# A transformer block on one core: the order of key units, values in two halves, and pinned row statistics

## The chip, the cores and the metric

The kernel runs on one core of one Trainium2 chip. The time is that of the device for one execution, in microseconds (us). Before the change it was run three times: 3664.93, 3666.43 and 3667.56 us, a median of 3666.43. A further execution was taken by the hardware profiler: 3665.12 us, of which 3663.4 us are the span that its trace covers.

A core has five engines that work through their own instruction streams in order and wait for one another by semaphores. TensorE (PE in the trace; PEld are its weight loads) multiplies matrices into banks of PSUM. VectorE (DVE) and ScalarE (ACT) work on rows of 128 partitions, GpSimd (POOL) as well, and SyncE (SP) here issues DMA transfers.

## The reference

The input h has 8 batch elements of 1024 tokens with 512 features, in float32. The block is an attention and a feed-forward layer, each between layer norms:

```python
x = h
x = x + layernorm(attention(layernorm(x)))
x = x + layernorm(ffn(layernorm(x)))

def attention(h):                      # 16 heads of 32
    q, v, k = split(h @ Wqvk)
    scores = q @ k.T                   # causal: a key after its query is masked
    return softmax(scores / sqrt(512)) @ v @ Wo

def ffn(x):                            # 512 -> 2048 -> 512
    hidden = x @ W1 + b1
    imag = w_imag * sin(theta + hidden * 0.1)
    phase = cos(theta) * w_real + sin(theta) * w_imag
    return relu(hidden + phase * imag * 0.1) @ W2 + b2
```

The means and variances of the layer norms are taken over the 512 features of a token (a row).

## The kernel before

**Outer order.** A loop runs over the 8 batch elements b. For each there are four attention groups g of four heads (`attention`, L867 to L971), then the end of the attention block for the second half of the tokens, interleaved with the feed-forward layer (`feed_forward`, from L1050). The feed-forward takes 8 steps: four quarters of the hidden features for each half of 512 tokens. Its products, the output projection's neighbours and the query and key projections of groups 1 to 3 use seven products in place of eight (Strassen and Winograd forms); POOL mixes operands for them, and mixed weights are kept in DRAM (`w1_mixed`, `w2_mixed`, `qk_mixed`). In the first batch element POOL also mixes these weights while attention runs.

**What sets the order.** Most instructions are issued through `in_order`, which pins an instruction in its engine's program order; one that goes through `id` instead, or through nothing, may be moved by the scheduler. The work is written as Python generators that issue a piece at each step: `advance(gen)` issues one piece, `finish(gen)` the rest. So the place of an `advance` call in the code is the place of that piece among the work of every engine that it uses. `staged(n, *stages)` gives a generator for n tiles through several stages, with tile t in stage k at step t + k. At each step the later stages come first.

**PSUM and buffers.** `psum()` hands out the 8 banks, preferring the one drained longest ago. The pool `pp` holds 24 tiles of 128x1024 f32 (keys, queries, values, weights of the softmax), `tmp` 5 tiles of 128x512, `wp` 18 tiles of weights.

**An attention group.** `project_qkv(b, g)` is a generator that makes a group's values, queries and keys. The values come in four pieces of two token tiles (`values`, L525 to L539: 8 matmuls to a tile of 128 tokens and 4 feature blocks in L530, then one ACT copy of 128x256 in L538). The first piece, `values(0)`, is issued in the previous group; the rest fills gaps in `find_maxima`, by the numbers in MAX_FILL. `find_maxima` computes the row maxima of the scores (L673 on PE, then L691 or L703 on DVE, with exponentials L723 on ACT). They are transposed (L913 copies the second half's to SBUF).

Then come the weights. For the two halves c of the queries, `KEY_UNITS[c]` lists units, each one or two blocks of 128 keys. For a unit, `weigh` puts minus the maxima (L779) and then the scores (L790) in PSUM on PE, takes the exponential on ACT (L805, two tiles) and, for a block on the diagonal of the causal mask, zeroes what lies above it with a select on POOL (L809). In the second half (c = 1) blocks 4 to 7 are those on the diagonal, so that the units (4), (5,7) and (6) need selects. The widths of queries are 512 for blocks 0 to 4, and 384, 256 and 128 for 5, 6 and 7.

A step behind it (`late`), PE multiplies the weights with the values (L828). In the second half the weights of all units are also added up on DVE in two tiles (`add_weights`, L857) into those of unit (0), and after the last unit PE sums these over the keys (L843) and ACT and DVE divide (L862 to L865). In group 3 the last two units are left out of the addition (`apart`) and summed on PE. At the last but one unit of c = 1 the group's projections are finished and the next group's first piece is issued (L916 to L919):

```python
if c and u == len(units) - 2:
    finish(work)
    work = projections(g + 1)
    advance(work)
```

Creating and starting a projection also allocates q, k and v in `pp` and issues its five weight fetches on SP.

**The norms.** `moments` (L309, L310) are the row statistics on DVE, `rstd_of` (L316, L317) two short POOL instructions, `normalised` (L328) one DVE instruction. For batch element b + 2, `measure_ahead` (L438 to L460) takes the statistics of the input x, tile by tile, during the last two feed-forward steps of b (by MEASURE). `norm1` uses them in group 2 of the element after. `finish_block` (L974 to L1046) projects the attention's output (L1005 on PE, a copy L1014 on ACT), takes its statistics, normalises and adds it to x (L1021), takes the statistics of x, scales it (L328 again, tile xn), transposes it on PE (L114) and mixes operands for the feed-forward on POOL (L1041). For the first half of the tokens this happens in group 3, for the second in the first three feed-forward steps, where `BETWEEN` says at which quarter-steps a stage is advanced.

**The feed-forward.** A step's hidden block comes from L1117 on PE, with additions on DVE (L1187) and copies on ACT (L1191, L1200). Then `wave_in` (L1138, L1143, L1144 on DVE, the sine L1145 on ACT) and `wave_out` (L1160, L1166 on DVE) form the wave, POOL mixes it (hm, L1233), and the second product (L1252 on PE) with additions (L1264, tile yb) makes the output. `end` (L1322 to L1351) finishes two tiles of output rows: POOL adds b2 (L1333), then in stages `measure`, `add` (L328 and L1343) and `store`. The last of these ends is left to the next element's group 0 and advanced there once a unit (`rest`).

Of the kernel before, what the change touches and what calls it, by code (L numbers as in the profile page):

```python
# [16 lines left out]
P = 128  # L17
# [15 lines left out]
def kernel(  # L33
# [14 lines left out]
    nc = tc.nc  # L48
# [257 lines left out]
    def moments(src, mv, keep=id):  # L306

        st = small.tile([P, 6], F32, tag="st", name="st", bufs=3)
        keep(nc.vector.bn_stats(st, src))  # L309
        keep(nc.vector.bn_aggr(mv, st))  # L310
# [127 lines left out]
    def measure_ahead(b, steps):  # L438


        xs = {}
        mvs = small.tile([P, NT, 2], F32, tag="mva", name="mva", bufs=1)
        rss = small.tile([P, NT], F32, tag="rsa", name="rsa", bufs=1)
        moments_ahead[b] = mvs, rss
        at = [sum(steps[:n]) for n in range(len(steps) + 1)] + [NT]

        def load(n):
            for t in range(at[n], at[n + 1]):
                xs[t] = load_again(b, t)

        load(0)
        load(1)
        yield True
        for n in range(len(steps)):
            for t in range(at[n], at[n + 1]):
                moments(xs.pop(t), mvs[:, t, :], in_order if b == 1 else id)
            if n + 2 < len(steps):
                load(n + 2)
            if n == len(steps) - 1:
                rstd_of(mvs, NT, rss)  # L460
            yield True
# [35 lines left out]
    def project_qkv(b, g):  # L497
# [24 lines left out]
            in_order(nc.scalar.activation(dst, pq, AF.Copy, scale=HALF_SCALE if n else -HALF_SCALE))  # L522
            drained(pq)

        def values(t0):  # L525
            pv = psum([P, 2, P])
            for t in (t0, t0 + 1):
                for kc in range(KC):
                    in_order(
                        nc.tensor.matmul(  # L530
                            pv[:, t - t0, :],
                            xnT[b, t // TPB][:, kc, (t % TPB) * P : (t % TPB + 1) * P],
                            w_of[b, g, 1][:, kc, :],
                            start=(kc == 0),
                            stop=(kc == KC - 1),
                        )
                    )
            in_order(nc.scalar.copy(v[b, g][:, t0 : t0 + 2, :], pv))  # L538
            drained(pv)  # L539

        def product(w, kc0, moving, dst, sign=1.0):
# [56 lines left out]
                values(t0)  # L598
                yield True

        values(0)
        yield True
        values(2)
        yield True
# [19 lines left out]
    MAX_LATE = (((7, 1),), ((7, 0),))  # L624


    MAX_FILL = ((2, 1, 1, 1), (1, 1, 1, 1))

    KEY_UNITS = (
        ((0,), (1, 3), (2,)),  # L630
        ((0,), (1,), (2,), (3,), (4,), (5, 7), (6,)),
    )

    def find_maxima(b, g, work, sums, more):
# [233 lines left out]
    def attention(b, wvT, after):  # L868
# [23 lines left out]
        for g in range(NG):  # L892
# [7 lines left out]
            for c in range(2):  # L900
# [3 lines left out]
                for u, keys in enumerate(units):  # L904
# [5 lines left out]
                    if at == 2:  # L910
# [2 lines left out]
                                parts_q[1], lambda *a: in_order(nc.vector.tensor_copy(*a))  # L913
                            )
                        )
                    if c and u == len(units) - 2:  # L916
                        finish(work)
                        work = projections(g + 1)
                        advance(work)  # L919
                    if first is None and (at < 2 or c and u >= len(units) - 2):  # L920
                        advance(more)
# [54 lines left out]
    def finish_block(b, half, wvT, x2T, mixed, out_w):  # L976
# [13 lines left out]

        def measure(t, source):
            mvs[t] = one_mv()
            moments(source, mvs[t][:, 0, :])
            if half:
                rss[t] = rstd_of(mvs[t], 1)

# [26 lines left out]
        def scale(t):  # L1023
            deviation(t)
            xns[t] = tmp.tile([P, D], F32, tag="tmp", name="xn")
            normalised(xns[t], x(t), mvs[t], rss[t])

        def transpose(t):
            transpose_rows(xns[t], x2T[half][:, :, t * P : (t + 1) * P], nc.scalar.copy)
# [20 lines left out]
    def feed_forward(b, x2T, mixed, before, between):  # L1050
# [14 lines left out]
            (1, 2, 1, 3),  # L1065
            (7,) * 6,
        )
        BETWEEN = ((0, 1, 2, 4), (1, 3), (3,))
        MEASURE = {STEPS - 1: 2, STEPS: 7}
        hids = {}  # L1070
        ahead = []
# [250 lines left out]
        def end(half, q, ybs):  # L1322
# [11 lines left out]

            def measure(t):
                mvs[t] = one_mv()
                last = (half, q) == (1, 1)
                moments(ybs[t], mvs[t][:, 0, :], in_order if last else id)
                rss[t] = rstd_of(mvs[t], 1)

            def add(t):
# [6 lines left out]
                if b + 1 < B:  # L1348
                    load_x(b + 1, i)

            return staged(len(ybs), measure, add, store)  # L1351

        def advance_ends(steps):
            for _ in range(steps):
# [116 lines left out]
```

## Time and profile before

| | |
|---|---|
| median of three runs | 3666.43 us (3664.93 to 3667.56) |
| the profiled execution | 3665.12 us, span 3663.4 us |
| granted TensorE clock, mean | 0.997 |
| instructions | 62,023 |
| busiest group of PE: L1117 from x2T, 2048 matmuls | 477.2 us |
| busiest group of DVE: L857, 400 additions | 423.7 us, mean 1.105 us |
| busiest group of ACT: L805, 640 exponentials | 566.1 us, mean 0.938 us |
| busiest group of POOL: L809, 512 selects | 291.7 us, mean 0.590 us |

A batch element in the middle takes about 451 us. The stretches of batch element 3, from the profile by windows (us from the start of the span; the busy times of the engines within each):

| stretch | window | PE | DVE | ACT | POOL | DMA share |
|---|---|---|---|---|---|---|
| end of the feed-forward before | 1381 to 1410.81 | 29.71 | 13.77 | 2.03 | 18.85 | 0.94 |
| group 0 | 1410.81 to 1468 | 56.76 | 44.94 | 34.27 | 32.04 | 0.25 |
| group 1 | 1468 to 1522 | 53.77 | 40.52 | 34.79 | 19.37 | 0.15 |
| group 2 | 1522 to 1575 | 52.77 | 42.43 | 37.21 | 20.47 | 0.15 |
| group 3 and first projections | 1575 to 1650 | 73.69 | 48.99 | 41.35 | 11.57 | 0.04 |
| entry of the feed-forward | 1650 to 1680 | 28.30 | 21.23 | 6.91 | 10.42 | 0.42 |
| feed-forward | 1680 to 1797 | 116.71 | 91.13 | 18.98 | 41.80 | 0.73 |
| its last two steps | 1797 to 1832 | 32.77 | 31.10 | 5.29 | 16.79 | 0.79 |

How to read it: a matmul's time runs to its modelled end and overlaps the next one's, so a stretch in which PE is busy nearly throughout can still hold matmuls that waited. In a line of the timeline the columns are start, duration, engine, line of the kernel, operation, tiles out<-in, shapes, how many of them in a row, and in brackets the idle time of the engine before them with what ended it. Four matmuls over 32 rows (the four heads of a group) run side by side on PE.

### The profile page before, as it was taken

The page shows a single profiled execution, that of the slowest core. Times are in us where ns is not written, and L with a number is a line of the kernel's source. Part 1 is how long each engine was busy: PE and PEld are TensorE (multiplying, and loading weights), DVE is VectorE, ACT ScalarE, POOL GpSimd, SP SyncE. Part 2 cuts the span into 40 slices and gives each one's busy share as a digit, 9 for nine tenths or more (in the row PEclk, how much of TensorE's full clock was granted, in tenths as well). Part 3 has the DMA queues.
Part 4 walks back from the last instruction along what each step waited for, and adds up shares of the span by engine and source line. Part 5 has one row for each costly group of instructions (what it writes and reads, how often), then busy time and mean ns, then how long its engine had stood idle before and what let it go on. Part 6 is the DMA issues. An engine that isn't in the chain of part 4 may idle for free.

```text
span 3663.4 us, 62023 instructions
## 1 busy us (share of the span) xinstructions
PE 3574.9 (98%) x22625; PEld 2342.6 (64%) x22625; DVE 2698.7 (74%) x5571; ACT 1449.6 (40%) x2780; POOL 1434.5 (39%) x1984
## 2 busy tenths in 40 slices
PE   8999999999999999999999999999999999999998
PEld 4447864478654786448864488544885548854587
DVE  5877768778686786767867677776777767777675
ACT  4553136621365214652146511464115642156310
POOL 5543453134541345313453234542344323443243
PEclk9999999999999999999999999999999999999999
DMA  4444761047610575105841068410683116720175
GB/s 139 159 142 121 247 204 47 21 137 246 196 47 16 153 252 173 53 10 168 262 148 53 13 181 268 126 53 17 197 275 105 47 35 198 262 81 19 52 220 194
DMA packets 312001, 488.83 MB, mean 133 GB/s; under 512 B 29904, under 2 KB 91408, under 8 KB 311696
## 3 DMA queue, kind: packets, MB, share of 16 engines
q1 hardware_dynamic: 309536, 483.02, 41.8%
q8 instruction: 180, 2.95, 0.3%
q10 hardware_dynamic: 2160, 1.84, 0.2%
q14 instruction: 125, 1.02, 0.1%
HBM read 451.71 MB, written 33.03 MB: 132 GB/s over the span
## 4 chain that ended last, share of the span: by engine, by line
PE 81%; DVE 11%; POOL 3%; ACT 2%; issue 1%; DMA 0%; SPq 0%; POOLq 0%; DVEq 0%; ACTq 0%
PE banks L1252 16%; PE banks L1117 15%; PE banks L545 8%; PE banks L673 8%; PE banks L828 6%; PE banks L790 6%; PE banks L530 6%; PE banks L1005 6%; PE banks L513 3%; PE banks L779 3%; PE banks L114 2%; DVE u L1144 2%; DVE hid L1160 2%; PE banks L843 1%; ACT w L805 1%
## 5 line engine op out<-in xcount | busy, mean ns | idle before, releaser
L805 ACT ACTIVATE w<-banks 128x1024 f32<-128x1024 f32 (+1 forms) x640 | 566.1, 938 | 259.4 <-PE banks L790 258.7
L857 DVE TENSOR_TENSOR w<-w 128x1024 f32<-128x1024 f32 (+3 forms) x400 | 423.7, 1105 | 182.8 <-PE banks L828 138.4
L809 POOL TENSOR_SCALAR_AFFINE_SELECT w<-w 128x256 f32<-128x256 f32 x512 | 291.7, 590 | 674.0 <-ACT w L805 666.2
L1117 PE MATMUL banks<-x2T,wm 128*128 128x256 f32 x2048 | 477.2, 381 | 28.2 <-DVE u L1187 13.6
L703 DVE CUSTOM_DVE_ANT_0 es<-banks,mask 128x128 f32<-128x128 f32 (+3 forms) x1024 | 432.2, 484 | 61.6 <-PE banks L673 61.6
L1252 PE MATMUL banks<-wm,hm 128*128 128x256 f32 x2048 | 470.3, 380 | 2.3 <-POOL hm L1233 2.3
L1145 ACT ACTIVATE u<-u 128x1024 f32<-128x1024 f32 x128 | 135.4, 1058 | 846.8 <-DVE u L1144 798.1
L1117 PEld LDWEIGHTS banks<-x2T,wm 128*128 128x128 f32 x2048 | 386.6, 190 | 91.1 <-DVE u L1187 16.8
L1252 PEld LDWEIGHTS banks<-wm,hm 128*128 128x128 f32 x2048 | 387.9, 190 | 56.5 <-POOL hm L1233 5.5
L691 DVE TENSOR_REDUCE mx<-banks 128x1 f32<-128x512 f32 (+1 forms) x384 | 309.8, 862 | 120.1 <-PE banks L673 119.8
L1233 POOL TENSOR_TENSOR hm<-hid 128x256 f32<-128x256 f32 x256 | 203.5, 795 | 448.8 <-DVE hid L1166 448.8
L1252 PE MATMUL banks<-wm,hid 128*128 128x256 f32 x1536 | 357.7, 379 | 0.0
L828 PE MATMUL banks<-w,v 128*32 128x512 f32 (+3 forms) x3072 | 322.9, 496 | 9.6 <-POOL w L809 9.6
L790 PE MATMUL banks<-q,k 32*128 32x512 f32 (+3 forms) x3072 | 330.9, 492 | 0.0
L673 PE MATMUL banks<-k,q 32*128 32x512 f32 (+3 forms) x3072 | 325.4, 513 | 0.4 <-DVE mx L703 0.2
L1252 PEld LDWEIGHTS banks<-wm,hid 128*128 128x128 f32 x1536 | 292.3, 190 | 39.2
L723 ACT ACTIVATE es<-es,mx 128x512 f32<-128x512 f32 (+3 forms) x512 | 279.7, 551 | 1.8 <-DVE mx L703 1.8
L530 PEld LDWEIGHTS banks<-wqvk,xnT 128*128 128x128 f32 x2048 | 238.5, 192 | 50.1 <-issue 25.4
L530 PE MATMUL banks<-wqvk,xnT 128*128 128x128 f32 x2048 | 260.3, 281 | 0.0
L673 PEld LDWEIGHTS banks<-k,q 32*128 32x128 f32 x3072 | 149.9, 185 | 146.9 <-DVE mx L703 66.9
L1117 PE MATMUL banks<-mix,wm 128*128 128x256 f32 x1024 | 241.9, 379 | 0.0
L1005 PE MATMUL banks<-wo,wvT 128*128 128x512 f32 x512 | 235.7, 601 | 3.2 <-DVE wvT L865 3.2
(135 smaller groups left out, 5074.1 us busy)
## 6 DMA issues: line engine op xcount, KB each, us to landing
wm<-w_mixed SPq DMA_DIRECT2D x1344, 256.0 KB, 3.1
xin<-in_L_attn_h_dram SPq DMA_DIRECT2D x112, 256.0 KB, 3.9
wqvk<-in_L_attn_Wqvk_dram SPq DMA_DIRECT2D x93, 256.0 KB, 5.4
out_dram<-x SPq DMA_DIRECT2D x64, 256.0 KB, 2.3
x<-in_L_attn_h_dram SPq DMA_DIRECT2D x60, 256.0 KB, 3.3
w_mixed<-w_t SPq DMA_DIRECT2D x56, 256.0 KB, 3.0
wmix<-qk_mixed SPq DMA_DIRECT2D x42, 256.0 KB, 5.1
wo<-in_L_attn_Wo_dram SPq DMA_DIRECT2D x32, 256.0 KB, 2.7
```

What stands on the lines that cost most here:

```text
L530: nc.tensor.matmul(pv[:, t - t0, :], xnT[b, t // TPB][:, kc, (t % TPB) * P : (t % TPB + 1) * P], w_of[b, g, 1][:, kc, :], start=(kc == 0), ...
L545: nc.tensor.matmul(pq, w[:, kc0 + kc, :], moving[:, kc, :], start=kc == 0, stop=kc == 1,)
L673: nc.tensor.matmul(scs[j // 2][:, j % 2, at : at + n], queries[r, i * P : (i + 1) * P], keys[r, k0 : k0 + n], start=True, stop=True,)
L691: nc.vector.tensor_reduce(out=mx[:, m], in_=sc[:, m, cols], op=ALU.min, axis=mybir.AxisListType.X,)
L703: nc.vector.tensor_tensor_reduce(out=es[:, m, cols], in0=sc[:, m, cols], in1=mask[:, HALF - n :], scale=1.0, scalar=FMAX, op0=ALU.add, op1 ...
L790: nc.tensor.matmul(sts[j // 2][:, j % 2, cols], all_keys[r, kb * P : (kb + 1) * P], all_queries[r, q0 : q0 + n], start=False, stop=True,)
L805: in_order(nc.scalar.activation(w[:, :, :width], st[:, :, :width], AF.Exp, scale=-1.0))
L828: nc.tensor.matmul(acc[r, HALF - n :], v[b, g][:, kb, r], weights[j // 2][:, j % 2, cols], start=first and k == 0, stop=last and k == len( ...
L857: in_order(nc.vector.tensor_add(t[:, :, q], t[:, :, q], w[:, :, cols]))
L1005: nc.tensor.matmul(y, wvT[:, kc, t * P : (t + 1) * P], out_w[kc], start=(kc == 0), stop=(kc == KC - 1),)
L1117: nc.tensor.matmul(bank[:, n, :], w[:, n, kc, :], moving[:, kc, :], start=first and kc == 0 and n == 0, stop=kc == 1 and n == 1, skip_grou ...
L1252: nc.tensor.matmul(region, a[:, n], w[:, n], start=start and n == 0, stop=last and n == 1, skip_group_check=True,)
```

## The change

- `measure_ahead` pins its statistics for every batch element, where before it did so only for b = 1.
- The first values piece of two token tiles, `values(0)`, becomes two pieces of one tile each, `values(0, 1)` and `values(1, 1)`. A projection has nine pieces instead of eight. MAX_FILL for group 0 takes three pieces first instead of two.
- The units of the second half are put in the order (0), (4), (1), (5,7), (2), (6), (3).
- The previous projection is finished, and the next one created and its first piece issued, after unit (0) of the second half. The second piece follows at the last but one unit.
- In `finish_block` the second half's statistics are pinned, and so is the scaling (L328) of that half. The stages between the feed-forward's pieces (`BETWEEN`) are put at other places over the first three steps.
- In `end` the first stage does nothing. The statistics are taken one step later, and are pinned always.

```diff
@@ -453,7 +453,7 @@
         yield True
         for n in range(len(steps)):
             for t in range(at[n], at[n + 1]):
-                moments(xs.pop(t), mvs[:, t, :], in_order if b == 1 else id)
+                moments(xs.pop(t), mvs[:, t, :], in_order)
             if n + 2 < len(steps):
                 load(n + 2)
             if n == len(steps) - 1:
@@ -522,9 +522,9 @@
             in_order(nc.scalar.activation(dst, pq, AF.Copy, scale=HALF_SCALE if n else -HALF_SCALE))
             drained(pq)
 
-        def values(t0):
-            pv = psum([P, 2, P])
-            for t in (t0, t0 + 1):
+        def values(t0, n=2):
+            pv = psum([P, n, P])
+            for t in range(t0, t0 + n):
                 for kc in range(KC):
                     in_order(
                         nc.tensor.matmul(
@@ -535,7 +535,7 @@
                             stop=(kc == KC - 1),
                         )
                     )
-            in_order(nc.scalar.copy(v[b, g][:, t0 : t0 + 2, :], pv))
+            in_order(nc.scalar.copy(v[b, g][:, t0 : t0 + n, :], pv))
             drained(pv)
 
         def product(w, kc0, moving, dst, sign=1.0):
@@ -598,7 +598,9 @@
                 values(t0)
                 yield True
 
-        values(0)
+        values(0, 1)
+        yield True
+        values(1, 1)
         yield True
         values(2)
         yield True
@@ -624,11 +626,11 @@
     MAX_LATE = (((7, 1),), ((7, 0),))
 
 
-    MAX_FILL = ((2, 1, 1, 1), (1, 1, 1, 1))
+    MAX_FILL = ((3, 1, 1, 1), (1, 1, 1, 1))
 
     KEY_UNITS = (
         ((0,), (1, 3), (2,)),
-        ((0,), (1,), (2,), (3,), (4,), (5, 7), (6,)),
+        ((0,), (4,), (1,), (5, 7), (2,), (6,), (3,)),
     )
 
     def find_maxima(b, g, work, sums, more):
@@ -913,9 +915,11 @@
                                 parts_q[1], lambda *a: in_order(nc.vector.tensor_copy(*a))
                             )
                         )
-                    if c and u == len(units) - 2:
+                    if c and u == 0:
                         finish(work)
                         work = projections(g + 1)
+                        advance(work)
+                    if c and u == len(units) - 2:
                         advance(work)
                     if first is None and (at < 2 or c and u >= len(units) - 2):
                         advance(more)
@@ -990,7 +994,7 @@
 
         def measure(t, source):
             mvs[t] = one_mv()
-            moments(source, mvs[t][:, 0, :])
+            moments(source, mvs[t][:, 0, :], in_order if half else id)
             if half:
                 rss[t] = rstd_of(mvs[t], 1)
 
@@ -1023,7 +1027,9 @@
         def scale(t):
             deviation(t)
             xns[t] = tmp.tile([P, D], F32, tag="tmp", name="xn")
-            normalised(xns[t], x(t), mvs[t], rss[t])
+            scaled = normalised(xns[t], x(t), mvs[t], rss[t])
+            if half:
+                in_order(scaled)
 
         def transpose(t):
             transpose_rows(xns[t], x2T[half][:, :, t * P : (t + 1) * P], nc.scalar.copy)
@@ -1065,7 +1071,7 @@
             (1, 2, 1, 3),
             (7,) * 6,
         )
-        BETWEEN = ((0, 1, 2, 4), (1, 3), (3,))
+        BETWEEN = ((0, 1, 2), (0, 2), (1, 3))
         MEASURE = {STEPS - 1: 2, STEPS: 7}
         hids = {}
         ahead = []
@@ -1334,8 +1340,7 @@
 
             def measure(t):
                 mvs[t] = one_mv()
-                last = (half, q) == (1, 1)
-                moments(ybs[t], mvs[t][:, 0, :], in_order if last else id)
+                moments(ybs[t], mvs[t][:, 0, :], in_order)
                 rss[t] = rstd_of(mvs[t], 1)
 
             def add(t):
@@ -1348,7 +1353,7 @@
                 if b + 1 < B:
                     load_x(b + 1, i)
 
-            return staged(len(ybs), measure, add, store)
+            return staged(len(ybs), lambda t: None, measure, add, store)
 
         def advance_ends(steps):
             for _ in range(steps):
```

On the engines this makes 32 matmuls fewer on PE (the sums of group 3: units (6) and (3) stand last there now), 32 ACT copies more (one of 128x128 twice for one of 128x256 in each of the 32 groups), and on DVE 240 additions of 128x1024 instead of 256, with 64 instead of 48 each of the forms of unit (5,7).

## The prediction

> **What bounds the kernel now.** I read the busy shares and the chain first, to see whether one engine sets the end.
>
> ```profile
> PE 3574.9 (98%) x22625; PEld 2342.6 (64%) x22625; DVE 2698.7 (74%) x5571; ACT 1449.6 (40%) x2780; POOL 1434.5 (39%) x1984
> PE 81%; DVE 11%; POOL 3%; ACT 2%; issue 1%; DMA 0%; SPq 0%; POOLq 0%; DVEq 0%; ACTq 0%
> ```
>
> TensorE (PE) is busy 98% and holds 81% of the chain at a granted clock of 0.997. The change takes no PE work away, so only the places where PE stands still can give anything. The list of PE's waits names them (line waited on, total us, times, longest):
>
> ```profile
> PE banks L1117 <- DVE u L1187: 15.9, 16, 1.7
> ...
> PE banks L828 <- POOL w L809: 9.6, 12, 2.4
> PE banks L1117 <- ACT p L1191: 9.2, 6, 1.5
> PE banks L779 <- ACT w L805: 8.7, 33, 1.0
> ```
>
> The whole list is 75 us, 9 of them one wait at the start. More stall hides inside busy matmuls that start late. Set against the same groups running freely, a batch element of 451 us loses some 14.5 us. The timeline of batch element 3 shows where, first at the end of its feed-forward (start, us, engine, line, idle before):
>
> ```profile
> 1805.76 1.03 PE L1252 MATMUL banks<-wm,hid 128*128 128x256 f32 x4
> 1808.31 3.72 PE L1117 MATMUL banks<-x2T,wm 128*128 128x256 f32 x16 [1.52 <-ACT p L1191]
> ...
> 1818.64 1.99 PE L1117 MATMUL banks<-x2T,wm 128*128 128x256 f32 x8 [0.57 <-DVE hid L1187]
> ...
> 1832.14 2.21 PE L1252 MATMUL banks<-wm,hm 128*128 128x256 f32 x9 [0.29 <-POOL hm L1233]
> ```
>
> With the late starts beside them PE loses 1.79, 0.83 and 0.56 us here, 3.2 in all. VectorE (DVE) at that time:
>
> ```profile
> 1799.19 0.69 DVE L309 BATCH_NORM_STATS2 st<-yb 128x6 f32<-128x512 f32 x1 [1.38 <-POOL yb L1333]
> ...
> 1802.53 0.69 DVE L309 BATCH_NORM_STATS2 st<-xin 128x6 f32<-128x512 f32 x1
> ...
> 1804.30 0.66 DVE L309 BATCH_NORM_STATS2 st<-xin 128x6 f32<-128x512 f32 x1
> 1804.88 1.76 DVE L1144 TENSOR_TENSOR u<-u,k 128x1024 f32<-128x1024 f32 x1
> ```
>
> Row statistics of y (waiting 1.38 for POOL) and of later inputs stand in front of the sine chain (L1138 to L1166) that PE waits for. Nobody needs those statistics soon. The second place is the start of the next element's group 0, where DVE's first maximum (L703) stands behind another statistic:
>
> ```profile
> 1411.74 0.70 DVE L309 BATCH_NORM_STATS2 st<-yb 128x6 f32<-128x512 f32 x1 [1.38 <-POOL yb L1333]
> ...
> 1412.57 0.26 DVE L703 CUSTOM_DVE_ANT_0 es<-banks,mask 128x128 f32<-128x128 f32 x1
> ```
>
> PE's 16 score matmuls at 1414.25 then take 3.10 us to the next group (1417.35) instead of 1.93. The third place is the end of each attention group; group 1:
>
> ```profile
> 1503.87 6.90 DVE L857 TENSOR_TENSOR w<-w 128x1024 f32<-128x1024 f32 x6 [5.12 <-PE banks L828]
> 1511.23 1.23 DVE L857 TENSOR_TENSOR w<-w 128x1024 f32<-128x1024 f32 x1 [0.45 <-POOL w L809]
> 1512.75 1.23 DVE L857 TENSOR_TENSOR w<-w 128x1024 f32<-128x1024 f32 x1 [0.30 <-POOL w L809]
> 1514.28 4.70 DVE L857 TENSOR_TENSOR w<-w 128x768 f32<-128x768 f32 x6 [0.30 <-POOL w L809]
> ```
>
> and POOL's selects there:
>
> ```profile
> 1510.79 0.41 POOL L809 TENSOR_SCALAR_AFFINE_SELECT w<-w 128x256 f32<-128x256 f32 x1 [11.30 <-ACT w L805]
> 1511.70 1.02 POOL L809 TENSOR_SCALAR_AFFINE_SELECT w<-w 128x256 f32<-128x256 f32 x1 [0.51 <-ACT w L805]
> ```
>
> The 14 additions take nearly all of 1503.87 to 1518.98; the weight sums (L843) need the last, and the next group starts on PE at 1520.02, 1.04 behind it. So the tail is a chain of additions, not of PE.
>
> **The change, part by part.** Durations are those of this profiled execution, 3665.12 us, 1.31 below the median and inside the runs' spread; I add the sum to the median.
>
> *Statistics at the feed-forward's end.* Those of the inputs (4 × about 0.85: L309 0.67 and L310 0.18, so 3.4 us of DVE) now follow the last wave stage, and those of y come a step later, behind POOL's addition of 1.27. The last hidden block is done at 1830.42 now. From 3.4 us and the 1.38 wait only what PE waits for counts, at most 3.2. The third stall is cured when the block comes 2.1 earlier; the first is partly ACT's copy of p (0.57, behind a 1.06 activation), so some 1 us remains. I take −2.1 (−1.0 to −2.6) in elements 0 to 5, and −1.0 in 6 and 7, which measure no inputs: −14.6.
>
> *Start of group 0.* No y statistic is ahead of the maxima; an input's may be, but that has no wait. 3.10 − 1.93 = 1.17, in 7 elements: −8.2. The cover is DVE being free: if the input statistics (8 × 0.85 at most) reach that far, the whole gain goes.
>
> *Group 0, second half.* Here the statistics, normalisation and addition that moved must still run: L309 and L310 0.88, L328 0.54, L1343 0.69, twice, less what overlaps and what stands here today. All 3.2 us now lie between additions. The first additions are those of unit (4), which need exponentials and selects: unit (0) leaves PE at 1446.60 and the additions start 3.76 later; with the values' first half (8 matmuls, about 1.0) and a select of 0.41 in between, 4.40. Then 13.55 of additions, 3.2 and gaps of 0.7: last addition at 21.85, weight sums at about 22.75, where today the next group starts at 20.57 (1467.17). +2.15 (1.9 to 2.4) in 7 elements: +15. What waits: the weight sums, then the next group's second values, first scores and maxima.
>
> *Groups 1 and 2.* The values' 1.0 us fills PE's stop behind unit (0) (0.9 with the late start), a gain; but products of units (4) and (5,7) now meet a select 0.41 to 1.02 long with less PE work ahead: +0.8 and +0.75. Group 1 from 1500.34: PE's own work 17.83, with these and 0.18 more 19.6, the additions' chain 18.5 + 1.04 = 19.5; late halves add up, so I take 20.1 against 19.68: +0.45 (0 to +0.8), 8 times, +3.6. In group 2 the next input's two normalisations (0.5 each) fall between the additions of (2) and (6): +0.85 (0 to +1.5), 7 elements: +6.1.
>
> *Group 3.* Units (6),(3) are summed by PE instead of (5,7),(6). That is 32 matmuls fewer in all, but 256 + 512 columns as 384 + 128 + 256 before: nothing. DVE adds 0.6 us more early on, hidden by some 2 us free between units. The normalised rows (L328) stand earlier in DVE's order, so the 0.69 wait at 1643.69 goes: −0.8 (−1 to +0.5), 8 times: −6.4.
>
> *Entry of the feed-forward.* Pinned statistics and scaling, with norm steps shifted, let the second step's u come at 1676.9 instead of 1678.54, but the third near 1682: of the 2.0 us stop, −0.55 (−1.2 to +0.5), 8 times: −4.4.
>
> *Costed at nothing.* 16 values matmuls as 8 and 8 take 1.98 either way. ACT has 32 more copies (0.37 for a full one; ACT is 40% busy). SP's five weight fetches per group go out five units earlier; in these stretches the DMA share is 0.15, nothing is queued behind them, and they land in a median 5.4 us. If no buffer were free then, SP would hold the stores and loads behind them. Element 0 has no earlier feed-forward and POOL mixes weights there: 0 ± 4.
>
> Sum: −14.6 − 8.2 − 6.4 − 4.4 + 15 + 3.6 + 6.1 = −8.9: **3657 us**. This case's own range is 3648 to 3668.
>
> A select takes 0.41 alone and 1.02 when it meets an addition (it ends 0.26 behind it). [...]
>
> **The rivals.**
> - *The tails cost little* (the additions slide into today's gaps). For it: DVE idles about 5 us before them in group 1. Against: the chain has under 1.1 us of gaps. Losses of 0.3 × 22 leave −27: 3639. Chance 0.20.
> - *Slower: selects and additions hold each other up.* Place: additions of (4) to (6) in groups 0 to 2. For it: under weight mixing in element 0 selects take 1.29 to 1.44 and additions 1.42 to 2.29. Against: in group 1 today additions beside selects take 1.23, like all others. Six additions by 1.42 − 1.22 give 1.2 a group, 22 groups, +26: 3683. It decides from 0.4 a group. Chance 0.26.
> - *The statistics were not the stall:* ACT's p and POOL's hm hold PE at the feed-forward's end. For it: the 1.52 wait names ACT. Against: that p waited for DVE's 1.76 addition. A gain of 0.5 instead of 2.1 or 1.0 there loses 10.6: 3668. Chance 0.14.
>
> **How the numbers follow.** 0.40 is left for my forecast. A measurement tells from no change about 0.2%, 7.3 us: faster is below 3659.1, slower above 3673.8. The forecast's case gives 0.24 faster and 0.16 same; the first rival 0.20 faster; the second 0.24 slower, 0.02 same; the third 0.06 same, 0.08 slower, since element 0 is open. Together 0.44, 0.24, 0.32. The range 3637 to 3684 leaves out the outer parts of the first two rivals, some 0.18.
>
> **What would show it.** Right: no L309 on y or inputs between L1138 and L1166 in the last two steps, and the 1.52 and 0.57 waits below 1; the score matmuls of group 0 near 2.0; group 0's last half some 2 us longer with its last addition near 21.8 from unit (0)'s end; in groups 1 and 2 PE waiting for selects before L828. Wrong: additions of 1.3 and more beside selects, PE waiting for values' copies, or an element that stays at 451 with the waits only renamed.

## The result and the profile after

The changed kernel takes 3700.49 us (median of 4 runs, 3699.00 to 3701.08), the kernel before 3666.98 (4 runs). The ratio is 1.0092, 95% interval 1.0074 to 1.0109: 33.5 us slower, where about 9 us faster were forecast, and outside the range. The page of the changed kernel, its span, its busy shares and its chain (lines of the kernel have moved by 2 to 6: L857 is L859, L809 is L811, L828 is L830, L1187 is L1193, L1252 is L1258):

```profile
span 3698.2 us, 61937 instructions
...
PE 3598.3 (97%) x22561; PEld 2332.5 (63%) x22561; DVE 2754.9 (74%) x5587; ACT 1455.0 (39%) x2812; POOL 1472.3 (40%) x1984
...
PE 81%; DVE 12%; POOL 3%; ACT 2%; issue 2%; DMA 0%; SPq 0%; POOLq 0%; DVEq 0%
```

PE has 64 matmuls less, eight in each element (the sums of group 3, for which 32 in all had been counted ahead of the run), and is busy 23 us longer; matmuls that wait count as busy in part, like the eight of unit (4) in group 1, shown below with 1.88 us recorded where others of the form have 1.07. POOL is busy 38 us longer with as many instructions, and DVE 56 us longer with 16 more: many of their instructions take longer each (POOL's 256 of hm from hid 231.0 us in all instead of 203.5, DVE's 256 of u from hid 179.7 instead of 147.4). The list of PE's waits after (waited on, total us, times, longest):

```profile
PE banks L830 <- POOL w L811: 22.1, 23, 1.6
PE banks L1123 <- DVE u L1193: 15.0, 16, 1.4
PE banks L1258 <- DVE hid L1172: 14.2, 8, 1.8
...
PE banks L1258 <- POOL hm L1239: 7.4, 8, 0.9
...
PE banks L781 <- ACT w L807: 3.1, 11, 0.6
```

Two waits of the list before are gone: that for ACT's p (9.2) and that for the hidden addition ahead of L1117 (5.4), and L781's stop behind unit (0) shrank from 8.7 to 3.1. In their place stands a new one on L1258 for DVE's hid (14.2), and the one for POOL's hm there grew from 2.3 to 7.4; both come once in each of the 8 elements. The wait for POOL's selects grew from 9.6 to 22.1. POOL in turn waits longer for DVE's statistics, before and after:

```profile
POOL rs L316 <- DVE mv L310: 163.3, 80, 5.0
```

```profile
POOL rs L316 <- DVE mv L310: 386.3, 119, 12.2
```

The stretches show where the time went. PE's matmuls of a stage are the same ones in both traces, so I took the time between the starts of the same matmuls (after minus before, us; element 0 apart, since POOL mixes weights there). "Products" are the 896 matmuls of an element's feed-forward, counted in order of time:

| stretch | element 0 | elements 1 to 7 | all | forecast |
|---|---|---|---|---|
| to the first weights of group 0 | −2.1 | −10.5 | −12.7 | −8.2 |
| group 0, second half | +0.5 | +23.2 | +23.6 | +15 |
| group 1, second half | +3.3 | +5.5 | +8.7 | +3.6 |
| group 2, second half | +4.7 | +8.0 | +12.7 | +6.1 |
| group 3 and the first projections | −1.1 | −7.7 | −8.8 | −6.4 |
| entry of the feed-forward (products 1 to 300 of 896) | +0.7 | +4.6 | +5.3 | −4.4 |
| end of the feed-forward (products 600 to 780) | +0.4 | +5.6 | +6.1 | −14.6 |
| sum | +6.3 | +28.6 | +34.9 | −8.9 |

The difference of the spans is 34.8. The largest miss is the end of the feed-forward. The stalls named in the prediction are gone there (−2.6 us up to product 740 in elements 0 to 5, −1.4 in 6 and 7), but +3.1 us stand behind them (2.04 at products 740 to 760, 1.04 at 760 to 780). PE in element 3:

```profile
1840.49 3.62 PE L1258 MATMUL banks<-wm,hm 128*128 128x256 f32 x16
1845.88 1.99 PE L1258 MATMUL banks<-wm,hid 128*128 128x256 f32 x8 [1.77 <-DVE hid L1172]
```

PE runs from the seventh step on without a stop, and then waits for the last wave. DVE, and then POOL, ahead of it:

```profile
1833.75 1.60 DVE L1144 TENSOR_SCALAR u<-hid,turns 128x512 f32<-128x512 f32 x2
1835.39 1.10 DVE L1149 TENSOR_SCALAR k<-u 128x1024 f32<-128x1024 f32 x1
1836.52 1.63 DVE L1150 TENSOR_TENSOR u<-u,k 128x1024 f32<-128x1024 f32 x1
1838.07 0.95 DVE L328 TENSOR_SCALAR yb<-yb,mv,rs 128x512 f32<-128x512 f32 x1
1839.05 1.10 DVE L1348 TENSOR_TENSOR x<-x,yb 128x512 f32<-128x512 f32 x1
```

```profile
1832.64 0.22 POOL L316 TENSOR_SCALAR rs<-mv 128x1 f32<-128x1 f32 x1 [4.56 <-DVE mv L310]
1832.94 0.57 POOL L317 TENSOR_TENSOR rs<-rs,mhalf 128x1 f32<-128x1 f32 x1
1833.48 0.73 POOL L1239 TENSOR_TENSOR hm<-hid 128x256 f32<-128x256 f32 x1
...
1837.03 1.71 POOL L1239 TENSOR_TENSOR hm<-hid 128x256 f32<-128x256 f32 x1
```

Two things are to be seen. A normalisation and addition of y (0.95 and 1.10) stand between the last two waves. And POOL stood idle 4.56 us at L316, which needs a statistic that DVE now takes late; the hm mixes behind it in POOL's queue start at 1833.48, beside the sine chain, and its three instructions take 1.60, 1.10 and 1.63 instead of the 0.88, 0.69 and 1.23 that they take alone (shown below in a run without L316 and L317). In the kernel before, POOL met the first of the two statistics after 1.49 us and the second without a wait, with its mixes between them:

```profile
1801.87 0.43 POOL L316 TENSOR_SCALAR rs<-mv 128x1 f32<-128x1 f32 x1 [1.49 <-DVE mv L310]
...
1803.02 0.72 POOL L1233 TENSOR_TENSOR hm<-hid 128x256 f32<-128x256 f32 x1
...
1807.19 0.21 POOL L316 TENSOR_SCALAR rs<-mv 128x1 f32<-128x1 f32 x1
```

Group 0's second half shows the same. First POOL's reciprocal deviation in the kernel before, where DVE is idle beside it; then, after the change, POOL and what PE meets.

```profile
1447.25 0.22 POOL L316 TENSOR_SCALAR rs<-mv 128x1 f32<-128x1 f32 x1 [1.45 <-DVE mv L310]
1447.56 0.57 POOL L317 TENSOR_TENSOR rs<-rs,mhalf 128x1 f32<-128x1 f32 x1
```

```profile
1468.72 1.10 POOL L316 TENSOR_SCALAR rs<-mv 128x1 f32<-128x1 f32 x1 [3.35 <-DVE mv L310]
1469.91 1.41 POOL L317 TENSOR_TENSOR rs<-rs,mhalf 128x1 f32<-128x1 f32 x1
1471.28 2.83 POOL L811 TENSOR_SCALAR_AFFINE_SELECT w<-w 128x256 f32<-128x256 f32 x4
```

```profile
1471.74 0.52 PE L830 MATMUL banks<-w,v 128*32 128x384 f32 x2 [1.64 <-POOL w L811]
...
1481.07 1.98 PE L845 MATMUL banks<-w,ones 128*32 128x512 f32 x8
```

The reciprocal deviation of a single column, 0.22 and 0.57 alone, takes 1.10 and 1.41 beside additions, and the selects of unit (5,7) stand behind it. In group 1, where no statistics are, only the order and the halved values are left (POOL, then PE):

```profile
1520.26 0.41 POOL L811 TENSOR_SCALAR_AFFINE_SELECT w<-w 128x256 f32<-128x256 f32 x1 [4.96 <-ACT w L807]
1521.17 1.02 POOL L811 TENSOR_SCALAR_AFFINE_SELECT w<-w 128x256 f32<-128x256 f32 x1 [0.51 <-ACT w L807]
```

```profile
1521.42 1.88 PE L830 MATMUL banks<-w,v 128*32 128x512 f32 x8
```

The eight matmuls of unit (4) take 1.81 us to the next group instead of 1.00: it starts at 1523.23, 1.04 behind the end of the second select (1521.17 + 1.02).

### The profile page after: what moved, and what is told of

Same layout as the page of the kernel before. It is cut to its first block, busy times and chain, and to the rows that moved or that the text cites. A ratio compares the mean times of both kernels' runs of the same rounds, so it can differ in the third digit from the quotient of the medians.

```text
span 3698.2 us, 61937 instructions
## 1 busy us (share of the span) xinstructions
PE 3598.3 (97%) x22561; PEld 2332.5 (63%) x22561; DVE 2754.9 (74%) x5587; ACT 1455.0 (39%) x2812; POOL 1472.3 (40%) x1984
## 4 chain that ended last, share of the span: by engine, by line
PE 81%; DVE 12%; POOL 3%; ACT 2%; issue 2%; DMA 0%; SPq 0%; POOLq 0%; DVEq 0%
PE banks L1258 16%; PE banks L1123 15%; PE banks L545 8%; PE banks L675 8%; PE banks L830 7%; PE banks L530 7%; PE banks L792 6%; PE banks L1009 6%; PE banks L513 3%; PE banks L781 2%; PE banks L114 2%; DVE u L1144 2%; DVE hid L1166 1%; DVE u L1150 1%; PE banks L845 1%
## 5 line engine op out<-in xcount | busy, mean ns | idle before, releaser
L859 DVE TENSOR_TENSOR w<-w 128x1024 f32<-128x1024 f32 (+3 forms) x416 | 429.9, 1076 | 217.1 <-POOL w L811 205.4
L811 POOL TENSOR_SCALAR_AFFINE_SELECT w<-w 128x256 f32<-128x256 f32 x512 | 289.8, 583 | 595.7 <-ACT w L807 518.1
L1258 PE MATMUL banks<-wm,hm 128*128 128x256 f32 x2048 | 471.1, 380 | 8.1 <-POOL hm L1239 7.4
L1258 PEld LDWEIGHTS banks<-wm,hm 128*128 128x128 f32 x2048 | 387.2, 190 | 66.1 <-POOL hm L1239 14.5
L1258 PE MATMUL banks<-wm,hid 128*128 128x256 f32 x1536 | 360.4, 380 | 15.5 <-DVE hid L1172 14.2
L830 PE MATMUL banks<-w,v 128*32 128x512 f32 (+3 forms) x3072 | 352.2, 499 | 22.5 <-POOL w L811 22.1
L1239 POOL TENSOR_TENSOR hm<-hid 128x256 f32<-128x256 f32 x256 | 231.0, 902 | 248.5 <-DVE hid L1172 248.5
L1258 PEld LDWEIGHTS banks<-wm,hid 128*128 128x128 f32 x1536 | 288.7, 190 | 60.3 <-DVE hid L1172 17.4
L530 PE MATMUL banks<-wqvk,xnT 128*128 128x128 f32 x2048 | 268.6, 283 | 0.0
```

Source lines behind the costliest of these rows:

```text
L530: nc.tensor.matmul(pv[:, t - t0, :], xnT[b, t // TPB][:, kc, (t % TPB) * P : (t % TPB + 1) * P], w_of[b, g, 1][:, kc, :], start=(kc == 0), ...
L830: nc.tensor.matmul(acc[r, HALF - n :], v[b, g][:, kb, r], weights[j // 2][:, j % 2, cols], start=first and k == 0, stop=last and k == len( ...
L859: in_order(nc.vector.tensor_add(t[:, :, q], t[:, :, q], w[:, :, cols]))
L1258: nc.tensor.matmul(region, a[:, n], w[:, n], start=start and n == 0, stop=last and n == 1, skip_group_check=True,)
```

## The experiments

My theory after the result: the loss comes from *end* (late statistics that hold POOL and stand in DVE's chain) and from the *order* (selects among plain units). Rivals: the early values, the pinned input statistics, the norms. First each part alone. All ratios below are against the kernel before, run on the same chip.

**The order of units alone.**

```diff
-((0,), (1,), (2,), (3,), (4,), (5, 7), (6,))
+((0,), (4,), (1,), (5, 7), (2,), (6,), (3,))
```

> The kernel before with the new order of units alone: (0), (4), (1), (5,7), (2), (6), (3); values in one piece at the last but one unit, norms and statistics as before. Theory 'order': the units with selects among plain ones make PE wait for the selects of (4) and (5,7) before L828, in every group; the changed kernel is 0.8 to 1.1 us a group longer there although the values' first half fills about 0.9 us behind unit (0), so the order alone should cost 1.5 to 2 us a group in groups 0 to 2 (24 groups): 36 to 48 us, 3702 to 3714. Rival 'halves': the tail is longer because the values were moved away from it; then the order alone is within 8 us of 3667.

3681.36 us, ratio 1.0044 (1.0029 to 1.0059): +16.0. Between theory and rival. Groups 0, 1 and 2 of elements 1 to 6 are about 1.0, 0.7 and 1.5 longer, element 0 adds 5.5, and group 3 with the first projections gives back 9.0, which I had left out. The order does cost, though in groups 0 and 1 about half of what I said.

**The values in halves alone** (`values(0, 1)`, `values(1, 1)`, the next projection after unit (0), MAX_FILL 3).

> The kernel before with the values' first piece in two halves and the next projection started after unit (0), nothing else. Theory 'order': the halves take up the stop behind unit (0) (0.9 us) but the tail hangs on the chain of additions, which starts about 0.4 later: -10 to +10 us, 3657 to 3677. Rival 'halves': moving 1 us of PE work away from the tail costs about 1 us a group, +25 us or more, 3692 and up.

3671.76 us, 1.0020 (1.0010 to 1.0029): +6.4, as the theory has it. The tails (second halves) of groups 0 and 1 are about 0.5 longer, group 2's 0.2: filling PE's stop behind unit (0) gave nothing, because the tail hangs on the additions, which in group 1 start 4.07 us behind unit (0) instead of 3.53.

**The inputs' statistics pinned, alone.**

```diff
-moments(xs.pop(t), mvs[:, t, :], in_order if b == 1 else id)
+moments(xs.pop(t), mvs[:, t, :], in_order)
```

> The kernel before with the input statistics of measure_ahead pinned for every element, nothing else. Theory 'end': the loss of 3.1 us per element in the last two feed-forward steps of the changed kernel comes from end's statistics being a step later; the inputs' statistics alone take 1.5 to 2.6 us per element away (6 elements), -9 to -16 us, 3651 to 3658. Rival 'inputs': pinning them is what made the new wait; +5 to +25 us, 3672 to 3692.

3658.14 us, 0.9981 (0.9971 to 0.9990): −7.2. Up to product 740 each of elements 0 to 5 is 1.2 shorter. A gain, a little short of the theory's 9 to 16.

**The late statistics of *end* alone** (the pin and the empty first stage).

```diff
-moments(ybs[t], mvs[t][:, 0, :], in_order if last else id)
+moments(ybs[t], mvs[t][:, 0, :], in_order)
...
-return staged(len(ybs), measure, add, store)
+return staged(len(ybs), lambda t: None, measure, add, store)
```

> The kernel before with end's statistics a step later and pinned, nothing else. Theory 'end': POOL's two small L316/L317 wait for the later statistics and hold back its hm mixes, which then run beside the sine chain and stretch it; with the normalisations between the last two waves about +3 us per element at products 740 to 780 (8 elements, +24), +2 in group 0's second half (7 elements, +14), less some 10 us at the start of group 0: +20 to +35, 3687 to 3702. Rival 'inputs': within 5 us of 3667, or below.

3710.71 us, 1.0124 (1.0107 to 1.0140): +45.4, more than the whole change. The place was right, the price was not. PE's stop at products 740 to 760 became 3.94 us in elements 0 to 5: five statistics of the inputs, left free, stand in the sine chain ahead of it (L309 on xin, from 1834.42 on in element 3). During the stop the granted clock fell. PE, and then windows of 2 us in element 3 (the busy time of each engine, then PEclk, the granted clock):

```profile
1840.23 2.75 PE L1252 MATMUL banks<-wm,hid 128*128 128x256 f32 x12
...
1850.37 5.49 PE L1252 MATMUL banks<-wm,hid 128*128 128x256 f32 x12 [3.94 <-DVE hid L1166]
```

```profile
1848.00:1850.00 2.00, 0.00 (x0) 0.00 (x0) 2.00 (x4) 1.06 (x1) 0.00 (x0) 0.79 0.99 332
1850.00:1852.00 2.00, 1.63 (x4) 1.37 (x5) 2.00 (x5) 0.00 (x0) 0.00 (x0) 0.50 0.97 346
1852.00:1854.00 2.00, 2.00 (x7) 1.56 (x6) 0.91 (x4) 0.00 (x0) 0.95 (x2) 0.50 0.50 129
1854.00:1856.00 2.00, 2.00 (x6) 1.63 (x5) 0.00 (x0) 0.00 (x0) 2.00 (x4) 0.50 0.59 197
1856.00:1858.00 2.00, 2.00 (x11) 1.73 (x10) 0.42 (x1) 0.37 (x1) 1.92 (x4) 1.00 0.56 170
```

For nearly 7 us the granted clock is 0.50, with six or seven matmuls to a window of 2 us instead of eleven.

**The norms alone** (both pins in finish_block, and BETWEEN).

> The kernel before with finish_block's pinned statistics and scaling and the other places in BETWEEN, nothing else. Theory 'sum': the changes add up by stage, and the entry of the feed-forward holds what the norms do: between products 48 and 300 the changed kernel has -0.44, -0.81, +0.70, +0.44, -0.44, +1.02 and +0.19 us per element, +0.66, times 8 is +5: 3667 to 3675. Rival (the prediction's step): the shifted norms let the second step's u come sooner, -4: 3658 to 3663.

3671.99 us, 1.0019 (1.0010 to 1.0028): +6.7, the theory's number. The stop at the second feed-forward step shrank, as forecast, and came back at the next product. In the changed kernel:

```profile
1694.14 1.99 PE L1123 MATMUL banks<-x2T,wm 128*128 128x256 f32 x8 [0.45 <-DVE u L1193]
...
1699.29 1.99 PE L1123 MATMUL banks<-mixl,wm 128*128 128x256 f32 x8 [1.43 <-DVE u L1193]
```

Before, these two were 1.70 and 0.29. A scaling, a statistic, a normalisation and an addition (1696.12 to 1698.55 on DVE) now stand in front of the next u.

**The changed kernel without *end*.**

> The changed kernel with end as before (statistics in its first stage, pinned only for the last). Theory 'end': the new wait at products 740 to 780 (+3.08 us per element) and most of group 0's longer half (+3.2, of which the order is 1.0) go, the start of group 0 becomes 1.2 longer again: 3700 - 25 - 15 + 8 is 3668, 3662 to 3676. Rival 'order': the tails are the loss, and without end's change the kernel stays above 3690.

3681.55 us, 1.0045 (1.0030 to 1.0060). Theory "end" in part: the new wait at products 740 to 780 is gone, and group 0's second half falls from +3.3 to +1.2. But the stalls before product 740 come back in part (−1.2 per element is left of −2.6), so removing the part gives 19 us and not 32.

**Two runs on the wait at the feed-forward's end.** The changed kernel without L316 and L317 in *end*, and without L328 and L1348 in one of its ends:

```diff
-rss[t] = rstd_of(mvs[t], 1)
+rss[t] = mhalf[:, :1]
```

> The changed kernel without the two POOL instructions L316 and L317 in end: the output rows are multiplied by a constant in place of the reciprocal deviation. Theory 'POOL held': POOL's queue stops at these until the later statistics are done, so that its hm mixes of the seventh step start 3 to 4 us late and run beside the sine chain, whose instructions then take 1.60, 1.10 and 1.63 us in place of 0.88, 0.69 and 1.23; without them the wait at products 740 to 780 falls from +3.08 to below +1.5 per element, -12 to -20 us: 3680 to 3688. Rival 'DVE inserted': the normalisation and addition between the last two waves (2.0 us) are the wait; then the wait stays at +2.5 to +3, 3695 to 3700.

```diff
 def add(t):
+    if (half, q) == (0, 1):
+        return
```

> The changed kernel without the normalisation L328 and addition L1348 of the end of the first half's second quarter: these output rows lack the feed-forward's part. Theory 'POOL held': the two DVE instructions between the last two waves are 2.0 us of a chain that is 5 us late; the wait at products 740 to 780 falls by at most 2 per element and the rest stays, 3684 to 3692. Rival 'DVE inserted': the wait goes altogether, +0.5 or less per element is left, -20 us and more, 3680 or below.

Without POOL's two instructions 3674.45 us, 1.0024 (1.0015 to 1.0033), 26 us below the changed kernel: the wait at products 740 to 760 is gone in all eight elements (−2.04 each), and group 0's second half is some 0.55 shorter. Its DVE and POOL in the seventh step:

```profile
1823.96 0.88 DVE L1144 TENSOR_SCALAR u<-hid,turns 128x512 f32<-128x512 f32 x2
1824.88 0.69 DVE L1149 TENSOR_SCALAR k<-u 128x1024 f32<-128x1024 f32 x1
1825.61 1.23 DVE L1150 TENSOR_TENSOR u<-u,k 128x1024 f32<-128x1024 f32 x1
```

```profile
1820.49 0.89 POOL L1239 TENSOR_TENSOR hm<-hid 128x256 f32<-128x256 f32 x1 [4.99 <-DVE hid L1172]
```

The mixes start ahead of the chain, and the chain runs unstretched. But without the two DVE instructions almost all of the wait at products 740 to 760 goes too: 3685.57 us, 1.0057 (1.0040 to 1.0074), −1.89 per element. PE at that place without POOL's two, and without DVE's two, neither with a stop ahead of it:

```profile
1833.85 2.79 PE L1258 MATMUL banks<-wm,hid 128*128 128x256 f32 x12
```

```profile
1839.14 2.00 PE L1258 MATMUL banks<-wm,hid 128*128 128x256 f32 x8
```

So neither theory was right alone. The last wave is some 2 us late; from that L1144 to the end of the first L1172 behind it DVE takes 12.5 us in the changed kernel (from 1833.75 on), 9.8 without POOL's two and 10.7 without its own two, so that either one taken away is about enough. Both expectations had treated them as alternatives. At products 760 to 780, +0.67 and +1.03 of the +1.04 stay; PE waits some 0.9 for the last hm there in all three kernels, 0.29 before, which neither run explains. And of the 26 us some 2 lie in element 0's attention, ahead of the first instruction that was left out.

**The order without the select of block 4.**

```diff
-if kb >= c * TPB:
+if kb >= c * TPB and (c, kb) != (1, 4):
     own.append(at)
```

> The new order of units alone (as in a_order), without the select of block 4 in the second half: masked keys of that block stay in the weights. Theory 'select late': unit (4) stands second, and PE's L828 for it waits for exponential and select with no products between; without the select 0.41 to 1.02 us of the wait go, 0.6 to 0.9 a group in groups 0 to 2 where the order alone cost 0.7 to 1.3: 3681 - 14 to - 22, 3659 to 3667. Rival 'wide end': the order costs because the last unit is 1024 wide instead of 512; then the selects don't matter, 3677 to 3682.

3661.50 us, 0.9988 (0.9979 to 0.9997), 20 us below the order alone: 0.82, 0.73 and 0.79 in groups 0, 1 and 2 of elements 1 to 7, and 6.5 in those of element 0. Theory "select late" holds; the wide last unit is not it. In group 2 some 0.7 of the order's 1.5 is left, without a run that explains it.

**The norms' pins without the new places** (with the inputs pinned).

> The inputs' statistics pinned (as in c_inputs, 3658) and finish_block's statistics and scaling pinned, with BETWEEN as before. Theory 'places': what e_norms lost (+1.0 us per element at products 150 to 200 and +0.7 and +0.4 at 80 to 120) comes from the other places in BETWEEN; the pins alone are then within 3 us of c_inputs, 3655 to 3661. Rival 'pins': the pinned statistics stand in front of the sine chain; then +5 or more, 3663 and up.

3664.89 us, 0.9998 (0.9989 to 1.0007), 6.8 above the inputs alone, the rival's side: the pins alone make the entry 0.67 longer per element, as much as pins and places together (0.66); element 6 alone has 2.1, beside a stretch of 3.4 us at a clock of 0.50. The places moved the loss about and added nothing to it; BETWEEN by itself was not tried.

**The last end started earlier in group 0** in the changed kernel, so that its statistics and one normalisation lie ahead of the additions:

```diff
 while len(quarters) > 1:
-    advance_ends(1)
+    if next(quarters[0], None) is None:
+        quarters.pop(0)
...
-return rest, len(KEY_UNITS[0])
+return rest, 1
```

> The changed kernel with the last end of an element advanced one unit of the first half earlier in group 0 (statistics with the third unit of the first half, one normalisation ahead of the additions, one between them, as in the kernel before). Theory 'additions set the tail': of the 3.3 us that group 0's second half is longer per element, the 1.2 of the order remain and some 2.0 go, in 7 elements: 3700 - 14, 3682 to 3690. Rival 'held selects': the statistics' reciprocal deviations on POOL hold the selects up wherever they stand; less than 0.7 per element goes, 3695 and up.

3685.25 us, 1.0053 (1.0038 to 1.0069): −15.2, and group 0's second half −2.1 to −2.3 per element, theory "additions set the tail".

**Inputs pinned and late *end* together.**

> The kernel before with the inputs' statistics pinned and end's statistics a step later and pinned (c_inputs and d_end together). Theory 'clock': d_end alone cost 45 us because the inputs' statistics, left free, were put into the late sine chain, PE stopped for 3.9 us and its clock then fell to 0.50 for some 7 us; with the inputs pinned the stop is 2 us as in the changed kernel and the clock stays: -3 us per element at products 740 to 760 in 6 elements and no half-clock stretch at the feed-forward's end, 3711 - 18 to - 28, 3683 to 3693. Rival 'sum': the two parts add up as they stand, 3711 - 7, 3701 to 3706.

3689.99 us, 1.0062 (1.0048 to 1.0075), where the two alone add up to 3704 (3666.2 + 45.4 − 7.2): the wait at products 740 to 760 falls from 5.1 to 2.0, and the half-clock stretch at the feed-forward's end is gone. A shorter one of 3.4 us remains in group 0, at a stop of 1.3 us behind stops of 0.2 and 0.7. The theory holds. One of the four executions took 3682.93 us at a mean clock of 0.996, the others 3689.68 to 3690.61 at 0.993.

**Versions that beat both kernels.** The early start of the last end, with the inputs pinned and nothing else of the change:

> The inputs' statistics pinned (as in c_inputs) and the last end of an element started only with the next element's group 0, one unit of the first half earlier than before: its first statistics stand neither ahead of the maxima nor, like its last normalisation, between the second half's additions. Theory 'additions set the tail': start of group 0 -1.2 us in 7 elements as in the changed kernel, the tail -0.6 to -1.2 instead of +3.3: 3658 - 8 - 4 to - 8, 3641 to 3647. Rival: the statistics delay the second half's maxima and what is gained is lost there, 3654 to 3662.

3645.33 us, 0.9946 (0.9933 to 0.9958). The start of group 0 is 1.16 shorter, its second half 0.66 to 0.89. DVE there:

```profile
1441.93 0.55 DVE L328 TENSOR_SCALAR yb<-yb,mv,rs 128x512 f32<-128x512 f32 x1 [1.00 <-POOL rs L317]
1442.52 0.69 DVE L1343 TENSOR_TENSOR x<-x,yb 128x512 f32<-128x512 f32 x1
1443.44 6.90 DVE L857 TENSOR_TENSOR w<-w 128x1024 f32<-128x1024 f32 x6 [0.24 <-PE banks L828]
```

The last normalisation ends in DVE's idle time, and six additions follow without a break. Moving group 2's normalisations likewise (`c and u < 2` for the last two units) did not help:

> As best_rest, and the next element's two last normalisations in group 2 advanced with units (0) and (1) of the second half instead of the last two. Theory 'additions set the tail': two instructions of 0.5 us leave the chain of additions at group 2's end for DVE's idle time ahead of it, -0.5 to -1.1 us in 7 elements against best_rest: 3634 to 3643. Rival 'cover': the transposes that come with them filled PE at the tail, and moving them costs what it gains: within 2 us of best_rest or above.

3650.82 us, 0.9960 (0.9948 to 0.9973): group 2 is 1.0 longer in elements 1 to 6, the rival's side. And the new order in group 3 only:

> best_rest with the new order of units in group 3 only. Theory 'order': in group 3, where DVE has no tail of additions (the last two units are summed on PE), the order alone gave -0.97, +0.43 and -0.54 us per element, -1.1 in all, times 8: 3645 - 9, 3635 to 3639. Rival: these gains belong to the order in the groups before; within 3 us of best_rest.

3637.40 us, 0.9923 (0.9911 to 0.9936), 28.8 below the kernel before: −0.97, +0.43 and −0.54 in every element, as the order alone had given there.

## Why the prediction was wrong

*End of the feed-forward (−14.6 forecast, +6.1).* This is the step that failed. "Nobody needs those statistics soon" is true of their values, and false of the queues: L316 and L317 wait for them in POOL's program order, and the hm mixes wait behind. I listed what a late instruction releases on DVE and not what is queued behind its reader on POOL. I also let the normalisations come a step later at no cost, though they then fall between the last two waves. Either alone would have cost next to nothing at products 740 to 760 (2.04 us together; 1.89 to 2.04 less when one is taken away). Without the held POOL the stretch is worth −1.8 in elements 0 to 5, close to the −2.1 I had for them: the gain was sized well, the price was missing.

*Entry (−4.4, +5.3).* The second step's stop shrank as said, but the third's grew by 1.1 and later ones by 0.8. I had seen the third come late and let the gain outweigh it. The pins alone lose, so there was no gain to weigh.

*Group 0 (+15, +23.2 in the same elements).* The mechanism was right, the size short. The last addition came 22.6 us behind unit (0) instead of the 21.85 that I had added up: POOL's small instructions, stretched to 2.51 from 0.79, held back a normalisation by 0.47 and the selects, and the additions took 14.0 where I had 13.55.

*Groups 1 and 2 (+9.7, +13.4 in elements 1 to 7).* Right in place: PE waits for selects at L830, and the run without one shows 0.73 to 0.82 for it. The gain behind unit (0) that I set against it did not come: the halves alone made these groups longer.

*Element 0 (0 ± 4, +6.3).* The loss is in groups 1 and 2, 8.0, beside POOL's weight mixing, where the rival "selects and additions hold each other up" had seen it. But part of it goes with the clock, which I had left out: it was 0.50 for 6.83 us from 219.59 on, in group 2, and the run without L316 and L317, the same program up to there, has no such stretch and is 2.2 us shorter in that group. No run separates the rest.

*Start of group 0 (−8.2, −10.5 in the same elements) and group 3 (−6.4, −8.8).* The first is right: late *end* alone gives −1.16 an element for the 1.17 forecast, and the other 0.3 comes only with the rest of the change and stays open. Group 3 is right by luck: its gain is the order's, which puts plain units where PE sums; it appears with the order alone (−1.1 an element) and not with the pins, so the reason I gave (the scaling earlier on DVE) is not the one.

The slower rival had the direction, with 3683 for another sum: the additions did not grow to 1.42 as a rule. Its mechanism, POOL and DVE side by side, also worked at the feed-forward's end (1.60, 1.10 and 1.63 on DVE for 0.88, 0.69 and 1.23), where I had not placed it. A select of 1.02 beside an addition is again what the changed kernel shows (1521.17), and in group 0 the two short POOL instructions went from 0.22 to 1.10 and from 0.57 to 1.41. The 1024-wide additions beside selects took 1.22 to 1.42 in group 1, against 1.23 in the kernel before, and the order alone cost 16 us.

## What to carry to other kernels

Before moving an instruction later, list who reads its result on every engine, and what stands behind that reader in its queue; a tiny reader can hold a long queue (here L316, 0.22 us itself, for which POOL stood idle 4.56 us ahead of the mixes). When two delays overlap, taking either away can remove the whole wait (here 2.04 and 1.89 us of 2.04), so try both before naming one. Work that nobody needs soon belongs where its engine is idle, here ahead of the additions (0.66 to 0.89 us less per element in group 0's second half) and not merely behind the chain it used to disturb.

## What the runs showed of the hardware

In element 3 of the run with late *end* alone PE stopped at 1846.43 for 3.94 us, and TensorE's granted clock fell at 1849.17. It was 0.50 for about 7 us, and 12 matmuls behind the stop took 5.49 us instead of 2.75, so the stop cost 2.7 us more than its length. In the run with the inputs pinned and late *end* together, after stops of 0.2, 0.7 and 1.3 us close together, it was 0.50 for some 3.4 us. In the changed kernel stops of 1.8 and 0.9 us at the feed-forward's end left it at 1.00, and behind the stops of 1.64 and 0.51 in group 0, the same in elements 1 to 7, it fell in elements 2 and 6 (at 1018.31 and 2837.61, for 3.41 us each) and in none of the others. So the lengths of the stops do not tell by themselves when the clock falls, and what decides it was not shown.

It also fell where PE counts as busy: in element 7 of the kernel before it was 0.50 for 10.24 us from 3384.11, and in that of the changed kernel for 10.24 us from 3417.88. 52 matmuls there take 11.63 us in both, while 16 of the same form take 2.00 in group 1 of element 3 of the kernel before, so that they seem to have waited within their recorded time.
